# A two-layer scan, attention and experts kernel: last turns in two parts, two batches' experts packed, small sums in PSUM

## The chip, the cores and the metric

The kernel runs on one core of one Trainium2 chip. What is compared is the device time of one launch, in microseconds (us), as a median of several executions. A traced execution gives the profile: when each instruction of the five engines ran, what it waited for, and which transfers were under way. The engines are called PE (matrix multiply), DVE (vector), ACT (scalar functions), POOL (GpSimd) and SP, which here only issues transfers. Each engine works through its own list of instructions in order; semaphores tie the lists together. All data is float32.

## What is computed

x has the shape (4, 384, 32, 32): 4 batches, 384 channels, 1024 positions. Layer 0 is a selective scan in four directions, layer 1 a windowed attention and a mixture of four experts:

```python
x = x + _L0_conv_ref(_gn(x), ...)          # group norm, then the scan layer
t = _to_tokens(x)                          # (4, 1024, 384)
t = t + _L1_attn_ref(_ln_t(t), ...)
t = t + _L1_ffn_ref(_ln_t(t), ...)
x = _from_tokens(t, x)

# the scan layer: positions by rows, by columns, and both reversed
xs = _cross_scan(x)
...
def step(h, inp):
    dtt, ut, bt, ct = inp
    dA = jnp.exp(dtt[..., None] * A)
    h = h * dA + (dtt * ut)[..., None] * bt[:, :, None, :]
    y = jnp.einsum('bkdn,bkn->bkd', h, ct)
    return (h, y)
...
# the experts: two of four for each token
topk_vals, topk_idx = jax.lax.top_k(probs, TOP_K)
...
h = jax.nn.gelu(jnp.einsum('bsd,edh->ebsh', x, w1) + b1[:, None, None, :], approximate=False)
y = jnp.einsum('ebsh,ehd->ebsd', h, w2) + b2[:, None, None, :]
out = jnp.einsum('bse,ebsd->bsd', masked, y)
```

The state has 16 values for each channel and direction, so a batch has 4 x 384 x 16 recurrences of 1024 steps. Attention has 6 heads of 64 and looks back 64 tokens. An expert is 384 to 1536 to 384.

## The kernel before

**A scan slot.** The scan is cut into turns, one for each batch and direction: 16 turns, four a batch, the directions in the order of `ORDER` (columns, columns reversed, rows, rows reversed). A turn has 3 channel tiles (`t`) of 4 blocks (`j`) of 32 channels; a block has four groups (`g`) of 4 states, so that 32 channels x 4 states fill the 128 partitions. One block and one group is a slot: 48 slots a turn, 768 in all. A slot is five steps on 128x1024 elements:

- `spread` loads the steps dt and dt*u of 32 channels, each row four times, from DRAM into `dts` and `dtu` (512 KB each, once for four slots), through SP.
- `times_b`, on POOL: z = spread of dt*u times the row of B. At most three slots ahead of the scan, with 7 buffers z.
- `decay`, on ACT: dA = exp(a * dt), into one of two dA buffers in PSUM.
- `scan`, on DVE: one tensor_tensor_scan over 1024 positions. Its result h goes over z or over dA.
- `times_c`: h times the row of C, on POOL where h is in z, on DVE where it is in dA. `scan` chooses: POOL, if the planner's clock of POOL is not more than 0.6 ahead of DVE's (`on_pool`).

`fold_y` sums over states on PE, for two blocks at once: 16 matmuls with `fold` (128x32) into ps_y, added to a row in DRAM (`ydr`). It gives the z buffers back.

**What feeds and follows it.** `group_norm(b)` normalizes batch b and projects it to the rows of dt, B and C; `time_steps` and `half_step` make softplus(dt) and dt*u for one channel tile at a time, at most 40 slots ahead. When all folds of a batch are in DRAM (`have.add(("scan", b))`), `tokens(b)` takes its eight tiles of 128 tokens, three at a time: y0, layer norm, gelu (ps_g), layer norm, q, k, v (ps_qk, ps_v), scores (ps_s), softmax, transposes (ps_p), ps_o, projection (ps_pr), and the experts' logits. Four tiles are a part; `route` then finds the two experts of each of its tokens, counts how many went to each expert, gives each token a row in `xsdr` by indirect transfers from POOL, and lists blocks of 128 rows with the expert of each. `SIZES` says how many blocks a part may list: 5 for the first of a batch, 14 for the second, 19 in all, since 2048 pairs of a token and an expert fill at most 16 + 3 blocks. `loads`, `hidden` and `output` run the blocks: 8 weight tiles of 576 KB each, 36 matmuls 128x128x128 (ps_hid), gelu on ACT, 12 matmuls with 384 columns (y_ff). When the 19 blocks of a batch are done, `combine(b)` gathers each token's two results (`cb<-ysdr`), weighs and adds them (ps_c) and writes the output.

**What sets the order.** Everything is a Python generator that is run once while the program is built. `Machine` keeps a planner's clock for each engine and a price for each instruction (`Engine.ask`), and always emits the one that could start first by its clock, with a bias: scan feed and tokens early, experts late. The order of each engine's list is fixed by this; waits on the chip are by semaphores. Weight tiles (`wts`, 8) and row tiles (`rows`, 10) are shared by tokens, experts and combining; `tokens` holds four weight tiles as long as it runs.

**Small steps.** `group_norm` keeps the means and deviations of its 3 columns in an SBUF tile `g`; `route` works on some 16 columns, most of them in a PSUM bank `ps_r`, some in SBUF (`p`, `r`, `total`, `done`, `start`).

The lines that the profile names are L148 for a single instruction (`Engine.run`) and L159 for one of a list (`Engine.all`), so groups go by tile names. The two that hold the choice of POOL or DVE, and when a batch's tokens may begin:

```python
on_pool = count_of["times"] >= min(s + AHEAD, NSLOT) and m.clock["pool"] < m.clock["dve"] + LEAD
...
folded[b] = folded.get(b, 0) + 2
if folded[b] == KG * NB:
    have.add(("scan", b))
```

Of the kernel before, what the change touches and what calls it, by code (L numbers as in the profile page):

```python
# [11 lines left out]
F32 = mybir.dt.float32  # L12
# [29 lines left out]
FULL = 2 * PT - NE + 1  # L42
SIZES = (FULL, 2 * NT + NE - 1 - FULL)
MB = max(SIZES)
SEG, SPARE = NT, NE * NT
# [91 lines left out]
class Engine:  # L137
# [23 lines left out]
    def ask(self, op, a, k):  # L161
# [25 lines left out]
        elif self.name == "act":  # L187
            cost = 0.08 + 0.00085 * n + 0.1 * sum(hasattr(k.get(v), "tensor") for v in ("bias", "scale"))
            cost += 0.19 if "accum_out" in k else 0.0
            table = TABLES.get(a[2]) if op == "activation" else None  # L190
        elif self.name == "pool":
            cost = 0.1 + 0.0022 * n
        elif self.name == "sp":
            cost = 1.5
        else:
            cost = 0.17 + 0.00198 * n if "scan" in op else 0.14 + 0.00105 * n
            if n < 256 and not any(v.space == PSUM for v in outs + ins):
                cost += 0.5
# [14 lines left out]
DMA_RATE, DMA_TIME = 0.38e6, 2.2  # L213


class Machine:
# [51 lines left out]
    def account(self, op, start):  # L268
# [18 lines left out]
        if op.size:  # L287
            self.dma = max(self.dma, end) + op.size / DMA_RATE
            end = max(end + DMA_TIME, self.dma + 1.0)
# [101 lines left out]
def conv_attn_hybrid(  # L391
# [16 lines left out]
    al_sb = const_load(alog, [P, KG, T, NS], "al_sb")  # L408
# [23 lines left out]
    minus = const.tile([P, P], F32, name="minus")  # L432
    nc.gpsimd.tensor_scalar(minus, ident, -1.0, None, ALU.mult)
# [47 lines left out]
    base_e = const.tile([P, NE], F32, name="base_e")  # L481
    a4 = const.tile([P, KG, T, JB, NG], F32, name="a4")

# [34 lines left out]
    own = tables[:, JB * P : JB * P + SG]  # L518
    nc.gpsimd.memset(sel_j, 1.0)
# [13 lines left out]
    xsdr = [dram.tile([(SPARE + 1) * P, D], F32, name="xsdr", tag=f"xs{n}", bufs=1) for n in range(2)]  # L533
    ysdr = [dram.tile([(SPARE + 1) * P, D], F32, name="ysdr", tag=f"ys{n}", bufs=1) for n in range(2)]
# [4 lines left out]
    ORDER = (1, 3, 0, 2)  # L539
# [3 lines left out]
    NSLOT = len(blocks) * NG  # L543
    SP = 2 * NG
    TS, IS = JB * NG, NB * NG
    AHEAD = 3
# [6 lines left out]
    def place_of(s):  # L553

        return s // SP * 2 + s % 2, s % SP // 2

# [14 lines left out]
    def constants():  # L571
# [5 lines left out]
        for j in range(JB):  # L577
# [4 lines left out]
                pv, sel_j[:, j, :], al_sb.rearrange("p k t n -> p (k t n)"), start=True, stop=True  # L582
# [17 lines left out]
        yield from dve.tensor_scalar(base_e, count[:, :NE], float(SEG), None, ALU.mult)  # L600

    def prepare():
# [23 lines left out]
        for xs in xsdr + ysdr:  # L626
            for mb in range(0, SPARE + 1, SEG):
                yield scans(n)
                n += 4
                k = min(SEG, SPARE + 1 - mb)  # L630
# [22 lines left out]
    def group_norm(b):  # L653
# [21 lines left out]
        g = rp.tile([P, 5, T], F32, tag="g", name="g", bufs=1)  # L675
        mean, g_mean, dev, g_rstd, g_off = (g[:, n, :] for n in range(5))
        yield from dve.tensor_copy(mean, mv[:, :, 0])
        gs = rp.tile([GROUPS, 2], F32, tag="gs", name="gs")
        ps = yield from banks.take("ps_gm", 0)
        for n, src in enumerate((mean, dev)):  # L680
            for t in range(T):
                yield from pe.matmul(
                    ps[:GROUPS, T : T + 1], gm[:, t, :], src[:, t : t + 1],
                    start=t == 0, stop=t == T - 1,
                )
            yield from dve.tensor_copy(gs[:, n : n + 1], ps[:GROUPS, T : T + 1])
            for o in range(T):
                yield from pe.matmul(
                    ps[:, o : o + 1], gt_sb[:, ts(o, P)], gs[:, n : n + 1], start=True, stop=True
                )  # L690
            if src is mean:
                yield from dve.tensor_copy(g_mean, ps[:, :T])
                yield from dve.tensor_tensor(dev, mean, g_mean, ALU.subtract)
                yield from dve.tensor_tensor(dev, dev, dev, ALU.mult)
                yield from dve.tensor_tensor(dev, dev, mv[:, :, 1], ALU.add)
        yield from dve.tensor_scalar(g_rstd, ps[:, :T], EPS, None, ALU.add)
        banks.give(ps)
# [985 lines left out]
```

## Time and profile before

| | |
|---|---|
| median of 3 runs | 3823.28 us (3820.04 to 3826.16) |
| the profiled execution | 3807.62 us, span 3805.9 us |
| busy PE, DVE, POOL, ACT | 3060.2, 2906.1, 2795.4, 2217.3 us |
| first scan to last fold | 59 to 3088 us |
| last fold to the end | 3088 to 3806 us |
| transfers | 947 MB, 249 GB/s in the mean |

The span is what the engines took from the first to the last instruction; 1.7 us of the profiled execution lie outside it. Groups are listed as line, engine, operation, output and inputs, shape and count, then busy time, the mean of one in ns, and the idle time of the engine just before them. A PE matmul in float32 is two records in the trace. The trace was also read by stage: the scan of a batch (four turns) begins at 59, 719, 1529 and 2324 us, and the last fold ends at 3088 us.

### The profile page before, as it was taken

How to read it: one execution, taken by the hardware profiler on the slowest of the kernel's cores; microseconds unless marked ns; L12 is line 12 of the kernel's file. 1: busy time of each engine (PE TensorE's matmuls, PEld its weight loads, DVE VectorE, ACT ScalarE, POOL GpSimd, SP SyncE). 2: the span in 40 equal slices, each digit the busy share in tenths (PEclk: the TensorE clock that was granted, in tenths of full speed). 3: DMA queues.
4: the chain of work that ended last, by engine and by line, in shares of the span. 5: the costliest groups of instructions: out<-in, count | busy, mean ns of one | idle time of the engine just before them, and what ended most of it. 6: DMA issues, size and time to landing. Idle time of an engine off the chain costs nothing. (4 is left out here: it accounts for less than half of the span.)

```text
span 3805.9 us, 50657 instructions
## 1 busy us (share of the span) xinstructions
PE 3060.2 (80%) x16090; PEld 1880.4 (49%) x16090; DVE 2906.1 (76%) x3290; ACT 2217.3 (58%) x4020; POOL 2795.4 (73%) x1464
## 2 busy tenths in 40 slices
PE   5565565587888798877778888887988989999998
PEld 2111110155654455534444555555655568877886
DVE  5999999988799999898888999988898952421001
ACT  4455455476676677766566677877766645432221
POOL 4999989898789787999898799988999940101001
PEclk8666676688798899977788899988999999999997
DMA  6776684534488899754387889665789874479995
GB/s 212 278 276 233 247 309 145 195 117 156 167 299 333 299 370 332 287 171 141 122 283 257 299 310 361 218 235 179 239 286 365 312 232 142 142 243 345 313 318 188
DMA packets 392907, 947.32 MB, mean 249 GB/s; under 512 B 50848, under 2 KB 174616, under 8 KB 392640
## 3 DMA queue, kind: packets, MB, share of 16 engines
q1 hardware_dynamic: 381032, 918.51, 68.9%
q0 software_dynamic: 8192, 25.17, 1.9%
q8 instruction: 128, 2.10, 0.2%
q14 instruction: 139, 1.14, 0.1%
q10 hardware_dynamic: 3416, 0.41, 0.1%
HBM read 780.03 MB, written 182.78 MB: 253 GB/s over the span
## 5 line engine op out<-in xcount | busy, mean ns | idle before, releaser
L148 POOL TENSOR_TENSOR z<-dts,bc 128x1024 f32<-128x1024 f32 x768 | 1791.1, 2358 | 143.8 <-PE ps_y L159 90.8
L148 ACT ACTIVATE dA<-dts,a 128x1024 f32<-128x1024 f32 x768 | 854.9, 1118 | 536.5 <-DVE z L148 521.7
L148 DVE TENSOR_TENSOR_SCAN dA<-dA,z 128x1024 f32<-128x1024 f32 x421 | 963.0, 2287 | 77.3 <-ACT dA L148 55.1
L159 PE MATMUL ps_y<-z,fold 128*32 128x512 f32 x3072 | 658.3, 722 | 318.0 <-POOL z L148 184.3
L148 POOL TENSOR_TENSOR z<-z,bc 128x1024 f32<-128x1024 f32 x347 | 813.6, 2358 | 80.3 <-DVE z L148 72.3
L148 DVE TENSOR_TENSOR_SCAN z<-dA,z 128x1024 f32<-128x1024 f32 x347 | 779.6, 2276 | 33.2 <-ACT dA L148 31.4
L159 PEld LDWEIGHTS ps_hid<-xbt,w_sb 128*128 128x128 f32 x5472 | 668.4, 198 | 139.5 <-issue 46.5
L159 PE MATMUL y_ff<-w_sb,hs 128*128 128x384 f32 x1824 | 691.1, 521 | 49.3 <-ACT hs L159 40.3
L159 PE MATMUL ps_hid<-xbt,w_sb 128*128 128x128 f32 x5472 | 690.8, 283 | 38.2 <-issue 10.3
L148 DVE TENSOR_TENSOR z<-dA,bc 128x1024 f32<-128x1024 f32 x421 | 514.2, 1221 | 18.4
L148 ACT ACTIVATE hs<-ps_hid,bb 128x128 f32<-128x128 f32 x912 | 273.6, 364 | 419.7 <-PE ps_hid L159 361.6
L159 PEld LDWEIGHTS y_ff<-w_sb,hs 128*128 128x128 f32 x1824 | 346.2, 202 | 309.4 <-ACT hs L159 72.9
L159 PEld LDWEIGHTS ps_y<-z,fold 128*32 128x32 f32 x3072 | 91.4, 117 | 678.0 <-POOL z L148 310.5
L148 POOL DMA_INDIRECT cb<-ysdr,idx x64 | 62.1, 970 | 338.0 <-DMA ysdr<-yb 259.0
L148 DVE COPY yb<-y_ff 128x384 f32<-128x384 f32 x24 | 13.4, 558 | 307.1 <-PE y_ff L159 297.0
L159 POOL TENSOR_TENSOR rn<-rn,half 128x1 f32<-128x1 f32 x96 | 52.8, 550 | 242.6 <-DVE rn L159 234.5
L148 POOL DMA_INDIRECT xsdr<-tks,idx x64 | 65.0, 1016 | 160.2 <-DMA xsdr<-tks,idx 66.7
L148 ACT ACTIVATE ed<-ps_dt,dtb_sb 128x512 f32<-128x512 f32 x192 | 123.1, 680 | 22.9 <-PE ps_dt L148 15.1
L148 ACT COPY ed<-ps_dt 128x512 f32<-128x512 f32 x96 | 56.1, 584 | 110.6 <-DVE ed L148 110.5
L148 PE MATMUL ps_dt<-xd,dtw_sb 12*128 12x512 f32 x180 | 108.3, 774 | 10.6 <-ACT tt L148 2.9
L159 PEld LDWEIGHTS ps_o<-v,pt 128*128 128x128 f32 (+1 forms) x720 | 104.6, 226 | 12.1 <-issue 2.3
L159 PE MATMUL ps_o<-v,pt 128*128 128x64 f32 (+1 forms) x720 | 109.0, 313 | 0.8 <-ACT v L148 0.5
(219 smaller groups left out, 3555.4 us busy)
## 6 DMA issues: line engine op xcount, KB each, us to landing
w_sb<-wl SPq DMA_DIRECT2D x608, 576.0 KB
dts<-dtr SPq DMA_DIRECT2D x384, 512.0 KB
bc<-xdr SPq DMA_DIRECT2D x128, 512.0 KB
dtr<-ed SPq DMA_DIRECT2D x192, 256.0 KB
yp<-ydr SPq DMA_DIRECT2D x96, 256.0 KB
ydr<-yp SPq DMA_DIRECT2D x96, 256.0 KB
ub<-udr SPq DMA_DIRECT2D x45, 512.0 KB
wl<-in_w_dram SPq DMA_DIRECT2D x32, 576.0 KB
```

The source lines that it names most:

```text
L148: return getattr(self.real, op)(*a, **k)
L159: getattr(self.real, op)(*a, **k)
```

## The change

Four things are changed, each told here with its lines.

1. **Last turns in two parts.** `ORDER` becomes (1, 3, 2, 0), so that the last turn of a batch runs forward over rows, and turns 7, 11 and 15 (`halved`: the last of batches two to four) are taken as two halves of 512 positions: all channel tiles and blocks for the first half, then all for the second. A slot is then two blocks of 32 channels side by side, 512 positions each; it has two loads, two exponentials and two scans, and in the first half the last value of each scan is copied to a `carry` tile, from which the second half starts. `have` now tells of halves, and a token tile waits for its own half only.

2. **Experts' blocks packed.** `PACKS` puts batches two and three together: their tokens' rows fill one set of blocks, so that 5 + 8 + 8 + 14 = 35 blocks are listed for both, 5 + 14 for each of the others. Both are combined when the 35 are done. The row buffers of the pack are twice as long.

3. **Small sums in PSUM.** In `group_norm` and `route` steps with two inputs in SBUF get one of them in PSUM.

4. **The planner's prices.** ACT, scans, POOL's powers, indirect transfers and small DVE steps with two SBUF inputs cost more in `ask` and `account`.

Besides, the first batch's softplus takes its sum with a negated second term, so that a negated identity isn't needed, and the A logs are loaded into a weight tile that is free at the start.

```diff
+PACKS = ((0,), (1, 2), (3,))
+PACK = {b: g for g, bs in enumerate(PACKS) for b in bs}
+SIZES = []
+for bs in PACKS:
+    for at in range(2 * len(bs)):
+        full = 2 * PT * (at + 1) + (NE - 1 if at == 2 * len(bs) - 1 else 1 - NE)
+        SIZES.append(full - (2 * PT * at + 1 - NE if at else 0))
...
-            cost = 0.08 + 0.00085 * n + 0.1 * sum(hasattr(k.get(v), "tensor") for v in ("bias", "scale"))
+            cost = 0.14 + 0.00085 * n + 0.1 * sum(hasattr(k.get(v), "tensor") for v in ("bias", "scale"))
...
-            cost = 0.1 + 0.0022 * n
+            cost = 0.7 if ALU.pow in a or ALU.pow in k.values() else 0.1 + 0.0022 * n
...
-            cost = 0.17 + 0.00198 * n if "scan" in op else 0.14 + 0.00105 * n
-            if n < 256 and not any(v.space == PSUM for v in outs + ins):
-                cost += 0.5
+            cost = 0.26 + 0.00198 * n if "scan" in op else 0.14 + 0.00105 * n
+            if n < 512 and "scan" not in op and sum(v.space != PSUM for v in ins) > 1 and not any(v.space == PSUM for v in ins):
+                cost += 1.2
...
-            end = max(end + DMA_TIME, self.dma + 1.0)
+            late = DMA_TIME if e != "pool" else SCATTER if str(op.outs[0].space).endswith("DRAM") else GATHER
+            end = max(end + late, self.dma + 1.0)
...
-    ORDER = (1, 3, 0, 2)
+    ORDER = (1, 3, 2, 0)
...
+    halves = [(c, t, j) for c in range(NH) for t in range(T) for j in range(0, JB, 2)]
+    halved = (7,11,15)
...
-            yield from dve.tensor_copy(gs[:, n : n + 1], ps[:GROUPS, T : T + 1])
+            yield from dve.tensor_copy(gs[:, n : n + 1], ps[:GROUPS, 3 * T + n : 3 * T + n + 1])
...
-                yield from dve.tensor_tensor(dev, mean, g_mean, ALU.subtract)
-                yield from dve.tensor_tensor(dev, dev, dev, ALU.mult)
-                yield from dve.tensor_tensor(dev, dev, mv[:, :, 1], ALU.add)
+                mm.tensor_tensor(off, mv[:, :, 0], g_mean, ALU.subtract)
+                mm.tensor_tensor(dev, mv[:, :, 0], g_mean, ALU.subtract)
+                mm.tensor_tensor(off, off, dev, ALU.mult)
+                mm.tensor_tensor(dev, mv[:, :, 1], off, ALU.add)
...
+                for o in range(2):
+                    r = slice(32 * (j + o), 32 * (j + o) + 32)
+                    yield from sp.dma_start(
+                        dst[:, ts(o, HB)],
+                        dtrs[i, t][c, r, ts(hf, HB)].unsqueeze(1).to_broadcast([32, SG, HB]),
+                    )
...
-            yield from act.activation(
-                da, spreads[n, 0], AF.Exp, scale=a4[:, turns[i][1], t, j, g : g + 1]
-            )
+            for o in range(1 if hf is None else 2):
+                c = slice(0, L) if hf is None else ts(o, HB)
+                yield from act.activation(
+                    da[:, c], spreads[n, 0][:, c], AF.Exp,
+                    scale=a4[:, turns[i][1], t, j + o, g : g + 1],
+                )
...
+        if hf == 0:
+            yield from eng.tensor_copy(kept(n, g), pairs(h)[:, :, HB - 1 : HB])
+        yield from eng.tensor_tensor(view(zs[s], hf), view(h, hf), rows_of(i, g, 1, hf), ALU.mult)
...
+            if hf is not None:
+                for o in range(2):
+                    c = ts(o, HB)
+                    initial = kept(n, g)[:, o, :] if hf else 0.0
+                    yield from dve.tensor_tensor_scan(h[:, c], da[:, c], z[:, c], initial, ALU.mult, ALU.add)
...
+        for c in range(NH):
+            if folded[b, None] == whole and (whole == KG * NB // 2 or folded.get((b, c), 0) == NB // 4):
+                have.add(("scan", b, c))
...
         def tile(a):
+            yield lambda: ("scan", b, a // PT) in have
...
-        mm.tensor_reduce(r, p, AX.X, ALU.max)
-        mm.tensor_tensor(pp, p, bcast_last(r, NE), ALU.subtract)
+        mm.tensor_reduce(rr, p, AX.X, ALU.max)
+        mm.tensor_tensor(pp, p, bcast_last(rr, NE), ALU.subtract)
...
-        left[b] = left.get(b, 0) + 1
-        if left[b] == sum(SIZES):
-            have.add(("experts", b))
+        left[g] = left.get(g, 0) + 1
+        if left[g] == 2 * NT * len(PACKS[g]) + NE - 1:
+            for b in PACKS[g]:
+                have.add(("experts", b))
...
-            yield lambda: b < KEEP or ("out", b - KEEP) in have
+            yield lambda: PACK[b] < KEEP or all(("out", c) in have for c in PACKS[PACK[b] - KEEP])
```

## The prediction

> **What bounds the kernel now.** I read the page's slices first, then busy time by stage, then the groups by line, then who waits for whom.
>
> ```profile
> PE   5565565587888798877778888887988989999998
> DVE  5999999988799999898888999988898952421001
> ACT  4455455476676677766566677877766645432221
> POOL 4999989898789787999898799988999940101001
> PEclk8666676688798899977788899988999999999997
> ```
>
> The right third tells most: VectorE and GpSimd are nearly full for about 32 of the 40 slices and then empty, while TensorE stays at nine tenths to the end. So there are two stages one behind the other. I cut them at the end of the scan and at the two routing sums of the last batch. Columns: busy us and number of instructions of PE, PEld, DVE, ACT and POOL, then granted clock, DMA share, GB/s.
>
> ```profile
> 59.00:719.00 660.00, 396.94 (x1056) 85.50 (x1056) 632.33 (x402) 336.30 (x393) 609.53 (x266) 0.68 0.69 245
> 719.00:1529.00 810.00, 673.18 (x3607) 419.36 (x3604) 722.98 (x797) 558.02 (x999) 684.42 (x346) 0.85 0.71 256
> 1529.00:2324.00 795.00, 623.74 (x3298) 382.21 (x3296) 712.91 (x803) 532.07 (x938) 714.86 (x368) 0.84 0.68 241
> 2324.00:3088.00 764.00, 658.66 (x3843) 428.89 (x3835) 689.02 (x770) 546.42 (x1001) 708.65 (x365) 0.93 0.77 266
> 3088.00:3276.00 188.00, 178.51 (x1215) 148.42 (x1214) 56.04 (x221) 86.54 (x242) 11.76 (x32) 0.97 0.48 151
> 3276.00:3378.00 102.00, 94.84 (x619) 78.64 (x618) 35.91 (x156) 42.40 (x112) 14.02 (x24) 0.95 0.58 187
> 3378.00:3500.00 122.00, 111.85 (x699) 90.98 (x699) 16.70 (x61) 29.15 (x96) 19.81 (x21) 0.94 0.94 335
> 3500.00:3700.00 200.00, 200.00 (x1231) 160.48 (x1232) 10.90 (x20) 48.15 (x159) 3.11 (x4) 1.00 0.93 317
> ```
>
> The first four rows are the four batches' scans (four turns each, 192 slots), 3027 us together: DVE and POOL about 90% each, PE 78%. From 3088 on PE does what is left: it is busy 93 to 100%, for 718 us. So a microsecond of PE work taken out of the second stage is worth nearly a microsecond; in the first, PE work is worth something only where the folds of z come late. The groups (busy us, mean ns | idle us before them, who ended it), of GpSimd:
>
> ```profile
> L148 POOL TENSOR_TENSOR z<-dts,bc 128x1024 f32<-128x1024 f32 x768 | 1791.1, 2358 | 143.8 <-PE ps_y L159 90.8 <-DMA dts<-dtr 34.5 <-issue 5.7
> ```
>
> and of VectorE, shape by shape:
>
> ```profile
> L148 DVE TENSOR_TENSOR_SCAN dA<-dA,z 128x1024 f32<-128x1024 f32 x421 | 963.0, 2287 | 77.3 <-ACT dA L148 55.1 <-POOL z L148 20.8 <-issue 1.1
> ...
> L148 DVE TENSOR_TENSOR z<-dA,bc 128x1024 f32<-128x1024 f32 x421 | 514.2, 1221 | 18.4
> L148 DVE TENSOR_TENSOR ps_dt<-ps_dt,ed 128x512 f32<-128x512 f32 x144 | 99.4, 691 | 10.3 <-ACT ps_dt L148 8.4
> ...
> L159 DVE TENSOR_TENSOR ps_r<-p,r 128x16 f32<-128x16 f32 x8 | 9.5, 1183 | 0.6
> ...
> L159 DVE TENSOR_TENSOR ps_r<-ps_r,r 128x16 f32<-128x16 f32 x8 | 1.5, 182 | 0.3
> ```
>
> These are the prices of a slot, and a comparison: the same 16 elements take 1183 ns when both inputs lie in SBUF and 182 ns when one is in PSUM. The waits of the scan stage:
>
> ```profile
> POOL z L148 <- PE ps_y L159: 92.0, 41, 8.6
> ...
> DVE dA L148 <- ACT dA L148: 55.1, 44, 4.3
> ...
> DVE z L148 <- ACT dA L148: 31.4, 30, 3.5
> ```
>
> **What the Trainium skill says.** "SBUF — State Buffer", section "Who interferes with whom": a VectorE instruction with two SBUF inputs contends with a GpSimd instruction that reads SBUF, and the later one waits. The trace agrees: ps_r<-p,r took 424 to 2316 ns in its six runs beside the scan and 183 ns in its two after it. "VectorE: DVE Perf Modes", section "The TRN2 errata — SBUF-src ops pay a fixed extra latency per instruction": the cost is per instruction, so halves cost more than a whole. The trace has no 512-element scan, but its multiplies agree: 2 x 691 - 1221 = 161 ns. "TensorE: Matmul & The Clock Gate", section "What's actually happening": a PE kept busy gets its full clock; here 0.68 in the first row and 1.00 in 3500:3700.
>
> **The change, part by part.** The counts come from setting the two programs' instruction orders side by side, engine by engine.
>
> *Tail, packed experts.* The diff's SIZES give 19 + 35 + 19 = 73 blocks of experts for 76: each batch alone rounds up with three spare blocks, the pair needs them once. The blocks of batches two and three are also nearer done when the scan ends: after the last fold the old order has 30 blocks' output sums (y_ff), the new one 23. A block is 36 ps_hid and 12 y_ff matmuls; after 3088 the trace has 254.3 us for 1044 and 256.9 us for 360 of these, so 0.244 and 0.714 us each. Gone: 252 x 0.244 + 84 x 0.714 = 121 us. Given back: both packed batches are combined there, 24 tiles for 16, so 48 more ps_c matmuls at 40.5/96 us: +20 us, and 8 transposes, +2.
>
> *Tail, last turn in two parts.* The first four token tiles of a batch may start when the first half of its last turn is folded. Of the last batch, three tiles stand ahead of the last fold up to their scores' inputs: 9 each of ps_y, ps_g, ps_x, ps_t, 27 each of both ps_qk, 6 ps_v, some ps_s, ps_p and ps_o go from the tail. Summing all 1864 matmuls that are left (2288 before) at the tail's own prices I get 604 us, against 741 us for the old list. The old list took 717.7 us (3088.2 to 3805.9; groups overlap at their seams), so 0.969 of its sum: 604 x 0.969 = 585 us. The tail loses 133 us. Against that stands filler: up to the last routing sum the old order has 8 blocks between the token tiles, the new 6, and the tiles' chains (norms over DVE, POOL, ACT) then show more. Unknown from the trace: at least 0; at most 50, if a fifth of the 249 us up to there goes idle, three times today's share. I take 15. Tail: -118 us.
>
> *Scan, VectorE.* 144 of 768 scans are now two of 512: nothing if all cost is per element, at most 46 us if the fixed part is twice the multiplies' 0.161, which is the nearest row and which I take: 144 x 0.161 = +23. The second halves read their start from a one-column SBUF operand: the row cb<-cb,gate,ps_c, which has such an operand too, takes 603 ns beside POOL and 614 after it, so no port wait; nothing. 41 copies of the end values on DVE at 154 ns (total<-ps_r): +6. 18 multiplies by C fewer at 1.221: -22. Small sums in PSUM: the 24 two-SBUF steps of group norm and routing in the scan stage took 43.8 us one by one; at 0.17 each they are 4: -40. Eight combine tiles fewer (605 + 551 ns): -9. Three tiles' fronts more: +12. Sum -30.
>
> *Scan, GpSimd.* 19 multiplies more at 2.358: +45; 31 end copies at 0.19 (as rn<-rn): +6; 16 gathers fewer at 0.97: -16; norms of three tiles: +4. Sum +39. C multiplies are handed to whichever of the two engines is behind, so the mean counts: (+39 - 30)/2 = +5, at 90% busy +6.
>
> *Scan, other queues.* ACT: 144 x (2 x 0.632 - 1.118) = +21, 51 more gelu inputs at 0.364 = +19, ten table loads at 1.283 = +13; it is 65 to 72% busy in turns 4 to 15, and hidden. SP: spreads become 144 loads of half the size for 72; no wait of SP for itself shows in POOL's z row beyond the start. PE: 6664 matmuls up to the last fold for 6405; turns 8 to 11 go from 1790 to 2027, where turns 12 to 15, with 2066, were the fastest of the three loaded stages (764 us). So PE work is hidden there, unless folds come late. The time steps' feed: all three row blocks of a halved turn are wanted in its first half; they are prepared 40 slots ahead, so nothing. For the finer pieces' hops I add 4. What truer durations in the ordering bring cannot be priced: at best the scan runs at 92.5% for 90% busy, 60 us of the 2369 in rows two to four (row one runs at 96%); at worst it costs what C or D below cost. I take nothing. Scan: +10.
>
> *Start and end.* The A logs' load moves behind the other constants on ACT, the first slot waits for the spread at 59 us; 0 to +5, taken 0. The last eight tiles' combine is as before.
>
> Sum: span 3805.9 - 118 + 10 = 3698. The profiled execution took 3807.6, the median of the runs is 15.7 above it. So 3698 + 1.7 + 15.7 = **3715 us**.
>
> **The rivals.** A (the forecast): the tail gives 118, the scan holds. For it: PE was full in the tail and its list is 19% shorter, whatever the clock does. Against: the scan is four fifths of the time and every order in it is new.
> B: the scan gains too, since small steps no longer wait for the port and the order fits the durations; 60 us, so 3655. For: DVE and POOL idle 10% though neither lacks work. Against: the POOL multiplies rise.
> C: folds come late where PE is denser. 259 more matmuls in the scan at 0.348 us (623.74/1790) are 90 us; if two thirds of that reach POOL through full z buffers (92.0 us of such waits today), 60 us: 3775.
> D, slower: the halved turns starve the scan. In turns 7, 11 and 15 each slot needs two exponentials from ACT, and now token fronts with their gelu table loads stand in ACT's queue in the same turns; behind a scan that waits are its multiply by C, the release of one of only two dA buffers, and PE's fold. A wait for dA lasts 86.5/74 = 1.17 us today. It decides from 0.75 us on each of the 144 slots, 108 us, or 92 slots that wait as long as today's mean; with all of them waiting it is 168 us, so 3715 + 168 = 3883, with three quarters 3841. For: such waits exist. Against: turn 5, with a full load of tokens, shows no such loss.
> That the change does nothing is excluded by the order: three tiles stand ahead of the last fold.
>
> **How the numbers follow.** A 0.57, B 0.22, C 0.13, D 0.08. A measurement tells about 0.2% (8 us) from no change; a sliver of C and D falls within it, 0.02. Faster 0.90, same 0.02, slower 0.08. A's own bounds are -15 and +35 in the tail, -20 and +30 in the scan; the range takes in B and C but for their outer ends: 3640 to 3795.
>
> **What would show it.** Last scan near 3095 and 600 us behind it; 73 blocks, 23 of them after; ps_r<-p in PSUM under 0.2 us; 512-element scans of 1.2 to 1.3 us; POOL z near 366 second multiplies. Wrong if the last scan ends after 3200, if turns 7, 11 and 15 grow by more than 20 us each beyond their token work, or if PE idles over 50 us between the last fold and the last routing sum.

## The result, and the profile after

The changed kernel takes 3758.7 us (median of 4 runs, 3749.3 to 3764.8) against 3821.7 us (4 runs, 3808.4 to 3826.2): 0.984 of the time, 95% interval 0.981 to 0.987. It is faster by 63 us; the forecast was 107. Between the two traced executions the difference is only 45 us (spans of 3805.9 and 3761.2 us): the one before lay 15.7 us under the median that the forecast used, the one after 4 us above its own. What follows is read from the traces. The slices after, to set beside those of before:

```profile
PE   5655565578788887998886887878888879998997
DVE  5999999999889877979898977898789976422001
ACT  4445454477677767776775666766678666432221
POOL 4999979998899878987998878888799995022001
PEclk8666676578799998988886888888999989999997
```

Look at DVE and POOL: their full stretches end about one slice later than before, and DVE's has more sevens in it (seven among slices 9 to 33, where before had one). The second stage is shorter. The same cuts as for the kernel before, at the first scan of each batch and at the last fold (from and to, length; then busy us and instructions of PE, PEld, DVE, ACT and POOL; clock, DMA share, GB/s):

```profile
59.00:717.00 658.00, 381.86 (x1050) 81.94 (x1048) 617.26 (x394) 336.79 (x391) 619.66 (x271) 0.67 0.76 263
717.00:1535.00 818.00, 672.92 (x3681) 422.23 (x3682) 709.03 (x885) 584.96 (x1083) 717.87 (x381) 0.87 0.72 254
1535.00:2371.00 836.00, 690.32 (x3715) 426.75 (x3713) 715.63 (x877) 581.95 (x1072) 714.00 (x376) 0.86 0.75 256
2371.00:3169.00 798.00, 674.72 (x3823) 434.02 (x3823) 683.28 (x817) 554.93 (x1046) 703.18 (x363) 0.88 0.71 247
3169.00:3761.00 592.00, 547.27 (x3424) 445.19 (x3420) 126.96 (x452) 180.71 (x523) 75.08 (x100) 0.94 0.72 240
```

The tail fell from 718 to 592 us. The scan stage grew from 3029 to 3110 us, in the three loaded batches from 810, 795 and 764 to 818, 836 and 798. Adding up DVE's busy time over the four scan rows gives 2725 us for 2757: DVE works 32 us less and the stage is 81 us longer, so it idles 113 us more. By turns, cut at DVE's scans (turn 15 ends with its last scan, some 5 us ahead of the last fold; the tail is the last fold to the end):

| us | before | after |
|---|---|---|
| turns 0-3 | 660 | 659 |
| turns 4-6 | 629 | 593 |
| turn 7 (halved) | 181 | 225 |
| turns 8-10 | 608 | 608 |
| turn 11 (halved) | 187 | 227 |
| turns 12-14 | 604 | 601 |
| turn 15 (halved) | 158 | 192 |
| tail | 718 | 592 |

The halved turns lost 44, 40 and 34 us, 118 together, and turns 4 to 6 gained 36. The prices of single instructions came as expected; the groups of VectorE, shape by shape:

```profile
L155 DVE TENSOR_TENSOR_SCAN dA<-dA,z 128x1024 f32<-128x1024 f32 x332 | 759.3, 2287 | 78.4 <-ACT dA L155 57.0 <-POOL z L155 15.5 <-issue 5.6
...
L155 DVE TENSOR_TENSOR z<-dA,bc 128x1024 f32<-128x1024 f32 x402 | 490.7, 1221 | 17.0 <-DVE dA L155 0.5
L155 DVE TENSOR_TENSOR_SCAN z<-dA,carry,z 128x512 f32<-128x512 f32 x86 | 105.3, 1267 | 11.4 <-ACT dA L155 11.4
L155 DVE TENSOR_TENSOR_SCAN dA<-dA,z 128x512 f32<-128x512 f32 x82 | 100.4, 1225 | 18.9 <-ACT dA L155 12.8 <-issue 4.8
...
L155 DVE TENSOR_TENSOR_SCAN dA<-dA,carry,z 128x512 f32<-128x512 f32 x58 | 74.6, 1286 | 27.6 <-ACT dA L155 21.1 <-issue 5.7
L155 DVE TENSOR_TENSOR_SCAN z<-dA,z 128x512 f32<-128x512 f32 x62 | 71.3, 1203 | 13.6 <-ACT dA L155 10.1 <-POOL z L155 3.5
...
L166 DVE TENSOR_TENSOR ps_r<-ps_r,p 128x16 f32<-128x16 f32 x16 | 2.9, 182 | 0.6
```

A half scan takes 1203 to 1286 ns where a whole one takes 2275 to 2287, and a 16-element step with one input in PSUM 182 ns, where ps_r<-p,r took 1183. The waits moved (waited for: us in total, times, longest):

```profile
POOL z L155 <- PE ps_y L166: 96.7, 44, 7.0
DVE dA L155 <- ACT dA L155: 90.8, 50, 8.8
DVE ed L155 <- ACT ps_dt L155: 67.1, 34, 8.7
DVE z L155 <- ACT dA L155: 43.0, 34, 6.3
```

POOL waits for folds about as long as before (96.7 us for 92.0), so folds did not come late. DVE waits for ACT's dA 134 us for 86, and for its softplus steps 67 for 27. That points to ACT; e12 below puts it to the test.

### The profile page after: what moved, and what is told of

It reads as the page before. It is cut to its first block, busy times and chain, and to the rows that moved or that the text cites. A ratio compares the mean times of both kernels' runs of the same rounds, so it can differ in the third digit from the quotient of the medians.

```text
span 3761.2 us, 50316 instructions
## 1 busy us (share of the span) xinstructions
PE 3002.3 (80%) x15769; PEld 1826.0 (49%) x15769; DVE 2870.2 (76%) x3467; ACT 2259.9 (60%) x4144; POOL 2843.6 (76%) x1513
## 5 line engine op out<-in xcount | busy, mean ns | idle before, releaser
L155 ACT ACTIVATE dA<-dts,a 128x1024 f32<-128x1024 f32 (+1 forms) x912 | 892.9, 983 | 478.5 <-DVE z L155 452.7
L155 DVE TENSOR_TENSOR_SCAN dA<-dA,z 128x1024 f32<-128x1024 f32 (+1 forms) x414 | 859.7, 2077 | 97.3 <-ACT dA L155 69.7
L155 POOL TENSOR_TENSOR z<-z,bc 128x1024 f32<-128x1024 f32 x366 | 858.4, 2357 | 96.3 <-DVE z L155 78.7
L155 DVE TENSOR_TENSOR_SCAN z<-dA,z 128x1024 f32<-128x1024 f32 (+1 forms) x354 | 727.8, 2087 | 37.4 <-ACT dA L155 31.5
L166 PEld LDWEIGHTS ps_hid<-xbt,w_sb 128*128 128x128 f32 x5256 | 646.6, 200 | 136.4 <-issue 50.1
L166 PE MATMUL y_ff<-w_sb,hs 128*128 128x384 f32 x1752 | 675.5, 527 | 44.6 <-ACT hs L166 35.0
L166 PE MATMUL ps_hid<-xbt,w_sb 128*128 128x128 f32 x5256 | 667.4, 285 | 41.1 <-DMA w_sb<-wl 9.7
L155 DVE TENSOR_TENSOR z<-dA,bc 128x1024 f32<-128x1024 f32 x402 | 490.7, 1221 | 17.0 <-DVE dA L155 0.5
L155 DVE SCALAR_TENSOR_TENSOR ed<-ps_dt,ed 128x512 f32<-128x512 f32 x96 | 65.3, 681 | 67.4 <-ACT ps_dt L155 67.1
L155 DVE TENSOR_TENSOR_SCAN z<-dA,carry,z 128x512 f32<-128x512 f32 x86 | 105.3, 1267 | 11.4 <-ACT dA L155 11.4
```

What stands on the lines that cost most here:

```text
L155: return getattr(self.real, op)(*a, **k)
L166: getattr(self.real, op)(*a, **k)
```

## The experiments

Twelve kernels ran. Time is the median of the timed runs, and the ratio to the kernel before is given as its 95% interval. When the last fold comes and how long the tail and the turns (4 to 6, 7 and so on) last is read from one traced execution each:

| | time, us | ratio | last fold | tail | 4-6 | 7 | 8-10 | 11 | 12-14 | 15 |
|---|---|---|---|---|---|---|---|---|---|---|
| e1 no halves | 3730.5 | 0.974-0.979 | 3039 | 698 | 589 | 181 | 597 | 190 | 608 | 152 |
| e2 whole tokens | 3780.1 | 0.988-0.993 | 3080 | 691 | 590 | 215 | 595 | 210 | 588 | 161 |
| e3 last only | 3750.7 | 0.981-0.986 | 3080 | 660 | 584 | 180 | 598 | 188 | 612 | 194 |
| e4 no packs | 3771.4 | 0.986-0.990 | 3172 | 599 | 592 | 230 | 602 | 229 | 610 | 189 |
| e5 no halves, old prices | 3752.8 | 0.980-0.985 | 3056 | 690 | 591 | 180 | 612 | 184 | 608 | 155 |
| e6 before, new prices | 3834.0 | 1.003-1.006 | 3101 | 716 | 617 | 178 | 612 | 200 | 605 | 162 |
| e7 before, sums in PSUM | 3746.7 | 0.978-0.984 | 3052 | 692 | 602 | 170 | 614 | 181 | 602 | 162 |
| e8 split spreads | 3718.5 | 0.970-0.977 | 3031 | 686 | 583 | 171 | 614 | 172 | 610 | 159 |
| e9 split engines | 3766.6 | 0.984-0.989 | 3072 | 700 | 588 | 194 | 607 | 203 | 595 | 163 |
| e10 LEAD 0.61 | 3758.6 | 0.983-0.987 | 3032 | 721 | 610 | 175 | 595 | 191 | 590 | 158 |
| e11 one pack of three | 3740.1 | 0.978-0.982 | 3029 | 709 | 599 | 173 | 595 | 187 | 602 | 153 |
| e12 whole exponentials | 3739.8 | 0.977-0.980 | 3156 | 587 | 588 | 224 | 606 | 225 | 604 | 188 |

The control first, because it says what the others are worth.

**e10: another order alone.** e1 with `-LEAD = 0.6` / `+LEAD = 0.61`.

> A control: the change without its halved turns, where only the margin by which GpSimd takes a multiply is 0.61 us instead of 0.60. No instruction's work changes, only the order that the planner finds. It says how far a last fold and a tail move by another order alone, and so which of the differences of the other runs carry a reading. The order's list for the tail says 714 us against 692. If orders matter little: tail 715 to 722, last fold 3030 to 3050, time 3745 to 3765. If they matter: single turns move by 10 to 20 us against the same version at 0.60 and the last fold by up to 20.

Against e1 the last fold moved by 7 us, single halved turns by up to 6, a group of three turns by up to 21, the tail by 23, the time by 28. (PE's list for the tail, the matmuls that the order leaves behind the last fold at the prediction's prices, had said 22 for the tail.) So a difference of some 20 to 30 us in the time of two versions shows nothing by itself here; this is one control, and another order may move more. Below I rest on the last fold, on all three halved turns going one way, or on larger differences.

**e1, e2, e3: what the halves do.** e1 is the changed kernel with no halved turn:

```diff
-    halved = (7,11,15)
+    halved = ()
```

> No turn is halved; packing, PSUM sums and new prices stay. In the changed kernel's trace the last fold is at 3168 us (3088 before), turns 7, 11 and 15 took 225, 227 and 192 us (181, 187 and 158 before), turns 4 to 6 593 (630 before). The order has 2215 matmuls behind the last fold, 692 us at the tail's prices. Theory 1 (half turns cost about 40 us each in the scan, whatever the reason, and prices and PSUM sums give about 35 in turns 4 to 6 and as much later): last fold near 3050, time 3740 to 3755, below the changed kernel or level with it. Rival (the scan stage is longer because PE holds more experts' work or because of the new prices, not because of the halves): last fold stays above 3120, time 3810 or more.

e2 halves the turns but lets a batch's tokens begin only when both parts are folded:

```diff
-            yield lambda: ("scan", b, 0) in have
+            yield lambda: ("scan", b, 0) in have and ("scan", b, 1) in have
```

> The three turns are halved, but a batch's tokens wait for both halves, so that no token front stands in a halved turn. Order: 692 us behind the last fold. Theory 1a (the halved turns are slow because tokens start in their middle: four weight tiles and the tiles' rows are loaded among the spreads, the experts' rows land late, PE waits in order and ACT and DVE behind it): turns 7, 11, 15 fall to 190, 195 and 165 us, last fold near 3060 to 3080, time 3755 to 3775. Theory 1b (halving itself is slow: two exponentials, two scans, copies and hops for each slot): the turns stay at 215 or more, last fold above 3120, time 3815 or more.

e3 halves only the last turn (`halved = (15,)`).

> Only turn 15 is halved. Order: 672 us behind the last fold, turns 8 to 11 hold 1720 matmuls as without halves (1981 in the changed kernel), two tiles' fronts ahead of the last fold. Theory 1: turns 7 and 11 back near 185 us, turn 15 near 190; last fold near 3085, time 3750 to 3765. If the gain of the tail came from the last batch's own early tiles, as the prediction had it, the tail would be near 600 us; the order says 672, so that most of it comes from turns 7 and 11.

Halves gain nothing. e1, without them, takes 3730.5 us, with an interval below that of the changed kernel; e10, also without them, takes 3758.6, as the changed kernel does. So whether they lose on the time is within the reach of an order. On the last fold they do lose: 3039 us in e1 and 3032 in e10 for 3169. Halving alone (e2 over e1) costs 34, 20 and 9 us in the three turns, of which turns 12 to 14 give 20 back, and leaves the tail about as it was: 41 us on the last fold, 50 on the time (33 between the two traces). Theory 1 of e1 came true on the last fold (3039 us, near 3050). Neither theory of e2 holds as it was put: both the halves and the fronts cost. Letting token fronts into the halved turns (changed kernel over e2) takes 99 us out of the tail and puts 89 in front of it, in turns 7 to 15. e3 shows the same exchange in one turn: 42 us more in turn 15, 38 less in the tail. So of the 106 us between the tails of e1 and the changed kernel some 38 come with turn 15, and the rest with turns 7 and 11. What busy time says of the exchange: e1 in its three last turns, and below it the changed kernel in its own.

```profile
1305.00:1486.00 181.00, 167.47 (x885) 99.10 (x883) 163.86 (x110) 132.61 (x222) 150.81 (x65) 0.94 0.93 348
2083.00:2273.00 190.00, 148.63 (x796) 87.06 (x796) 176.94 (x190) 119.30 (x198) 173.56 (x84) 0.86 0.80 291
2881.00:3033.00 152.00, 135.22 (x777) 83.36 (x775) 144.22 (x84) 98.77 (x160) 151.47 (x67) 0.94 0.81 293
```

```profile
1311.00:1535.00 224.00, 184.05 (x995) 113.47 (x994) 173.50 (x205) 158.92 (x307) 180.40 (x99) 0.92 0.86 289
2144.00:2371.00 227.00, 181.79 (x939) 110.68 (x935) 176.82 (x209) 157.32 (x302) 172.37 (x94) 0.89 0.79 264
2971.00:3163.00 192.00, 156.70 (x901) 100.82 (x901) 156.03 (x181) 126.45 (x253) 166.64 (x93) 0.89 0.72 234
```

Before halving, DVE is busy 91 to 95% of these turns, PE 78 to 93% and POOL 83 to nearly 100%. There is little room for more work. After it no engine reaches 88%: in the three turns ACT has 92 us more to do, PE 71, POOL 44 and DVE 21, and they last 120 us longer. The rest is waiting.

**e4: packs.** `PACKS = ((0,), (1,), (2,), (3,))` in the changed kernel.

> Each batch lists its own blocks again (76), the rest as changed. Order: 599 us behind the last fold (585 with packs), 2098 matmuls in turns 12 to 15 for 2024. Theory: packing is worth about 14 us of the tail and the scan hardly changes: last fold 3160 to 3185, time 3765 to 3790. Rival (packing is worth its three blocks of 17 us): 3800 or more. Second rival (packing worth nothing, since 16 combines are put into the tail): 3750 to 3762.

The tail is 599 us for 592, the last fold 3172 for 3169, the time 3771.4 for 3758.7. The pack is worth some 13 us, less than an order moves; the 126 us of the tail do not come from it.

**e5, e6, e7: what made turns 4 to 6 shorter.** e5 is e1 with the old prices and DMA times in the planner, e6 the kernel before with the new ones. The lines of e6 for DVE; those for ACT, POOL's powers and the transfers are the change's own:

```diff
-            cost = 0.17 + 0.00198 * n if "scan" in op else 0.14 + 0.00105 * n
-            if n < 256 and not any(v.space == PSUM for v in outs + ins):
-                cost += 0.5
+            cost = 0.26 + 0.00198 * n if "scan" in op else 0.14 + 0.00105 * n
+            if n < 512 and "scan" not in op and sum(v.space != PSUM for v in ins) > 1 and not any(v.space == PSUM for v in ins):
+                cost += 1.2
```

e7 is the kernel before with nothing but the small sums of `group_norm` and `route` in PSUM, of which the first lines are

```diff
-        g = rp.tile([P, 5, T], F32, tag="g", name="g", bufs=1)
-        mean, g_mean, dev, g_rstd, g_off = (g[:, n, :] for n in range(5))
+        g = rp.tile([P, 3, T], F32, tag="g", name="g", bufs=1)
+        dev, g_rstd, g_off = (g[:, n, :] for n in range(3))
```

> The change without its halved turns, with the prices of small steps and DMA waits that the kernel before had. Question: turns 4 to 6, which hold no halved work, took 629 us before, 593 after and 589 in the version without halves. What took the 36 to 40 us out: the prices (another order of the same work), or the small sums left in PSUM? Theory P (prices, which my prediction set at nothing): turns 4 to 6 go back to 620 to 635 and turns 8 to 10 with them; last fold 3070 to 3090 against 3039, tail 690 (the order's own list says 684, against 692 with the new prices), time 3765 to 3785. Theory S (sums in PSUM): turns 4 to 6 stay at 585 to 598, last fold 3035 to 3050, time 3725 to 3745.

> The kernel before with nothing but the new prices in the ordering. The complement of the run without them. Theory P (the prices made turns 4 to 6 shorter): turns 4 to 6 near 590 to 600, last fold 3040 to 3060, tail 718 as before or a little less (the order's list 714 against 718), time 3755 to 3785. Theory S (the sums): turns 4 to 6 stay at 620 to 635, last fold 3080 to 3100, time 3800 to 3830, no change.

> The kernel before with nothing but the small sums of the norm and of the routing left in PSUM. Theory S: turns 4 to 6 near 590 to 600, as in the changed kernel, last fold 3040 to 3055; the order's list for the tail says 681 against 718, so time 3730 to 3765. Theory P: turns 4 to 6 stay at 620 to 635, last fold 3075 to 3095, and only the tail's list (681) pays: 3775 to 3800.

The sums did it: e7 alone takes 36 us off the last fold and 71 off the time. DVE's busy time ahead of the last fold falls from 2758 to 2707 us, POOL's rises from 2718 to 2731. The gain does not hang on one order: the six versions with these sums and whole scans (e1, e5, e7, e8, e10, e11) have their last folds at 3029 to 3056 us and take 3719 to 3759 us; the two without the sums, the kernel before and e6, have 3088 and 3101 and take 3822 and 3834. Turns 4 to 6 alone (27 us in e7, where the control moved such a group by 21) and the tail (26 us, control 23) would not show it. With the old prices turns 4 to 6 stay at 591. The prices alone make the kernel before no faster (0.4% slower), their 12 us in turns 4 to 6 come back as 13 in turn 11; e5 and e1 differ by less than an order moves.

At 3746.7 us e7, one part of the change, is as fast as the whole (3758.7), within what an order moves.

**e8: are the halved loads slow?** e1, with the spreads of turns 7, 11 and 15 loaded in two column halves. The expectation speaks of dt's spreads alone; the edit has no such condition and halves those of dt*u too, so that the trace has 144 loads of 256 KB, as many as the changed kernel:

```diff
+                for h in range(2 if i in (7, 11, 15) else 1):
+                    cc = ts(h, HB) if i in (7, 11, 15) else slice(0, L)
+                    n_c = HB if i in (7, 11, 15) else L
+                    yield from sp.dma_start(
+                        dst[:, cc],
+                        dtrs[i, t][c, 32 * j : 32 * j + 32, cc].unsqueeze(1).to_broadcast([32, SG, n_c]),
+                    )
```

> The change without its halved turns, where only the spreads of the first multiplier (dt) in turns 7, 11 and 15 are loaded by two DMAs of 512 columns instead of one of 1024: 48 issues and 48 halves more, the same bytes, no scan halved. Question: turns 7, 11 and 15 lost 34, 20 and 9 us by halving alone. Theory D (the transfers: pieces of 2 KB instead of 4, twice the issues in SP's queue): this version loses 15 to 30 us in turn 7 and 8 to 18 in turn 11 against 181 and 190, time 3750 to 3775. Theory E (the engines' own halves: ACT's two exponentials, DVE's two scans, the carry, and POOL's added multiplies): turns 7, 11 and 15 within 8 us of 181, 190 and 152, time 3722 to 3745.

Turns 7 and 11 came out shorter, not longer (171 and 172 for 181 and 190), turn 15 by 7 longer, turns 8 to 10 by 17. The theory of slow small loads fell. At 3718.5 us this is the fastest version that ran, but its interval overlaps that of e1, and by the control the difference can be the order's.

**e9: are the halved instructions slow?** e1, with scans and exponentials of these turns in two halves each, and nothing else halved. The lines of the scan; the exponentials are divided in the same way:

```diff
-                yield from dve.tensor_tensor_scan(h, da, z, 0.0, ALU.mult, ALU.add)
+                for o in range(parts):
+                    c = ts(o, L // parts)
+                    initial = h[:, HB - 1 : HB] if o else 0.0
+                    yield from dve.tensor_tensor_scan(h[:, c], da[:, c], z[:, c], initial, ALU.mult, ALU.add)
```

> The change without its halved turns, where each exponential of ACT and each scan of DVE in turns 7, 11 and 15 is made in two instructions of 512 columns (the second scan starts from the first one's last column): the same blocks in the same order, no carry, loads of 1024 columns, and every result as before. Added from the durations of the trace: 48 x (2 x 0.70 - 1.12) = 13 us for ACT and 48 x (2 x 1.27 - 2.28) = 12 us for DVE in each of the three turns. Theory E (the halves on the engines cost what halving cost, 34, 20 and 9 us in turns 7, 11, 15): these turns grow by 12 to 30 us each over 181, 190 and 152, last fold 3065 to 3100, time 3740 to 3775 (the order's list for the tail is 681 against 692). Theory O (what costs is the other order of a halved turn: two columns' halves, rows for two blocks at once, fronts and waits that come another way): at most 8 us each, last fold 3030 to 3060, time 3715 to 3745.

Turns 7, 11 and 15 grew by 13, 13 and 11 us, the last fold by 33. The half scans of e9:

```profile
L155 DVE TENSOR_TENSOR_SCAN dA<-dA,z 128x512 f32<-128x512 f32 x158 | 198.7, 1258 | 26.3 <-ACT dA L155 21.4 <-POOL z L155 2.4
L155 DVE TENSOR_TENSOR_SCAN z<-dA,z 128x512 f32<-128x512 f32 x130 | 160.3, 1246 | 5.1 <-ACT dA L155 3.0
```

288 of them take 359 us, and 144 whole ones at 2.28 would take 328: 31 us of DVE time, nearly all of the 33. Theory E holds at its lower end, and of the 41 us that halving puts on the last fold this is most. The run halves the exponentials too, and ACT has 41 us more to do ahead of the last fold than in e1, so it does not part DVE's share from ACT's. That DVE's counts is argued from e1, where DVE was busy 91 to 95% of these turns and ACT 63 to 73%.

**e12: is ACT the pace of the halved turns?** The changed kernel with each engine's order kept, where ACT makes a halved slot's decay in one exponential:

```diff
-                yield from act.activation(
-                    da[:, c], spreads[n, 0][:, c], AF.Exp,
-                    scale=a4[:, turns[i][1], t, j + o, g : g + 1],
-                )
+                call = (da[:, c], spreads[n, 0][:, c], AF.Exp), dict(scale=a4[:, turns[i][1], t, j + o, g : g + 1])
+                yield act.ask("activation", *call)
...
+                elif o:
+                    act.real.activation(da, spreads[n, 0], AF.Exp, **call[1])
```

> The changed kernel with its halved turns, token fronts and packs, and each engine's order of work kept instruction for instruction, except that ACT makes the decay of a halved slot in one exponential of 1024 columns instead of two of 512 (with the first block's scale for both, so the second block's decays are left out). It takes 48 x (2 x 0.70 - 1.12) = 13 us from ACT in each of turns 7, 11 and 15 and touches nothing else. Question: which engine's queue sets the pace of the halved turns, where DVE waited for ACT's dA and dt 29, 33 and 20 us. Theory ACT (ACT's one queue, which holds exponentials, dt steps and the token fronts' steps with two buffers for dA, is what the scan waits for): each halved turn gives back 9 to 15 us of 225, 227 and 192, last fold 3125 to 3145 against 3169, time 3715 to 3735. Theory PE/DVE (the halved scans on DVE, or PE's queue with its waits for loads, set the pace; ACT's lateness is only what came last): at most 5 us each, last fold 3155 to 3170, time 3745 to 3765.

(The A of this input is the same for all channels, so both blocks have the same scale and, unlike what the expectation says, nothing is left out.) The three turns:

```profile
1305.00:1529.00 224.00, 187.74 (x1012) 116.67 (x1010) 174.08 (x206) 148.61 (x261) 183.14 (x100) 0.91 0.85 289
2134.50:2359.00 224.50, 180.99 (x941) 110.07 (x939) 177.30 (x209) 146.18 (x254) 172.58 (x93) 0.90 0.79 268
2963.00:3151.00 188.00, 155.68 (x902) 100.87 (x903) 155.91 (x181) 115.47 (x207) 165.73 (x93) 0.90 0.73 240
```

ACT is relieved of 10 to 11 us in each and the turns last 224, 225 and 188 us for 225, 227 and 192. Theory ACT fell as far as the second exponentials go; ACT's other steps in these turns, those of the token fronts, no run took out. The time itself is 19 us lower than the changed kernel's, more than the other theory allowed; the traces place 7 of it in these turns, and the other differences (5 in turns 4 to 6, 5 in the tail, where the two kernels do the same) are not explained.

The waits, added up over the three turns, say where the relief went:

| us | e1 | e2 | after | e12 |
|---|---|---|---|---|
| DVE waits for ACT | 23 | 65 | 92 | 91 |
| ACT waits for PE | 32 | 70 | 111 | 138 |
| PE waits for transfers | 10 | 22 | 57 | 54 |

With less to do, ACT waited longer for PE, and DVE as long for ACT as before. ACT was the last to arrive; the waits fit that it stood behind PE, but no run shows it.

PE's own waits by what was waited for, in turn 15 of the changed kernel, and then of e2:

```profile
PE ps_xb L166 <- DMA xb<-xsdr: 14.5, 3, 8.2
PE ps_y L166 <- POOL z L155: 6.8, 4, 3.0
PE ps_y L166 <- DMA tt<-in_x_dram: 6.7, 1, 6.7
```

```profile
PE ps_y L166 <- POOL z L155: 14.3, 9, 3.1
PE y_ff L166 <- ACT hs L166: 3.9, 3, 1.4
PE ps_xb L166 <- DMA xb<-xsdr: 3.1, 1, 3.1
```

With token fronts in the turn PE stands 21 us for two loads, 3 without. The one of xb is issued among those of wq, wk and wv, 576 KB each. That fits the 31 us that fronts add to turn 15, but no run took these loads away, and turn 11 shows no such growth (4.9 us for xb, as in e2). What holds up the fronts there stays open.

**e11: a better pack?** e8 (its halved loads are again those of both spreads) with `PACKS = ((0,), (1, 2, 3))`.

> A version that may beat both kernels: no halved turns, dt's spreads of turns 7, 11 and 15 loaded in two halves (as in the run that had 3718 us), and the experts' blocks of batches one, two and three in one pack instead of two. Two blocks' worth of padding less after the last fold: the order's list for the tail says 627 us against 681. If the pack works as the other packs did (12 us for the change's pack by the run without packs, 54 here by the list): tail 630 to 640, last fold 3020 to 3050, time 3655 to 3690. Rival: the pack holds batch two's blocks back until batch three's routing, they pile up behind the last fold in spite of the list, or a larger segment makes the gathers wait: tail above 665, time above 3700.

The rival came true: the tail is 709 us for 627 by its list, though only 70 blocks are listed for 73. The first 300 us of the tail of e11 and of e8:

```profile
3029.00:3130.00 101.00, 89.20 (x542) 72.06 (x543) 31.96 (x122) 37.47 (x106) 8.88 (x24) 0.87 0.29 89
3130.00:3230.00 100.00, 81.31 (x501) 70.20 (x501) 44.79 (x201) 40.19 (x114) 15.57 (x28) 0.79 0.21 70
3230.00:3330.00 100.00, 82.76 (x542) 68.94 (x541) 21.52 (x100) 28.43 (x83) 9.25 (x12) 0.90 0.60 216
```

```profile
3031.00:3130.00 99.00, 90.72 (x600) 74.63 (x600) 24.35 (x95) 37.56 (x110) 5.19 (x14) 0.97 0.56 177
3130.00:3230.00 100.00, 96.06 (x691) 81.36 (x690) 44.86 (x193) 53.84 (x139) 10.21 (x24) 1.00 0.52 164
3230.00:3330.00 100.00, 90.49 (x600) 77.03 (x598) 33.15 (x145) 37.67 (x102) 15.41 (x24) 0.93 0.61 195
```

In the first 200 us of e11's tail far less is loaded than in e8's (89 and 70 GB/s for 177 and 164), and PE does fewer matmuls. It idles 48 us in the 300, for 22 in e8, at a granted clock of 0.79 to 0.90. Experts' work between the token steps, the filler, is missing, and the token steps' matmuls are slower as well (ps_t 332 ns for 277 in e8, ps_pr 309 for 276), those of the experts not (ps_hid 282 for 288).

## Why the prediction was half right

*The total.* 3758.7 us lies in the range, with some luck. By spans the forecast missed by 63 us (3761 for 3698), by medians by 44, because the traced executions lay on different sides of their medians. The tail came as forecast, the scan stage 71 us worse.

*Tail, -118 us: right in size.* Measured -126. PE's list for the tail and its length agree within 19 us in eleven versions out of twelve:

| us | before | after | e1 | e2 | e3 | e4 | e5 | e6 | e7 | e8 | e9 | e10 | e11 |
|---|---|---|---|---|---|---|---|---|---|---|---|---|---|
| by the list | (fitted) | 585 | 692 | 692 | 672 | 599 | 684 | 714 | 681 | 681 | 681 | 714 | 627 |
| measured | 718 | 592 | 698 | 691 | 660 | 599 | 690 | 716 | 692 | 686 | 700 | 721 | 709 |

The 15 us for thinner filler did not come. From the last fold to the last routing sum PE idles 15 us (3169 to 3414 us), and idled 17 in that stretch of the kernel before (3088 to 3379), far from the 50 that would have spoken against the forecast:

```profile
3088.00:3379.00 291.00, 274.35 (x1840) 228.06 (x1839) 92.46 (x380) 128.94 (x353) 25.78 (x56) 0.96 0.52 164
3169.00:3414.00 245.00, 230.27 (x1551) 189.92 (x1547) 92.42 (x362) 106.08 (x283) 46.29 (x70) 0.97 0.59 186
```

The cause was named wrong. The text gave most of the gain to the packed experts and the rest to three fronts of the last batch. e4 shows the packs nearly without part in it: what did it is the token fronts in the halved turns. They stand ahead of the last fold themselves and start the experts earlier (23 blocks are left for e2's 27.7; with packs and no halves, in e1, it is also 27.7, and without packs, in e7, 28.0), and that is the 99 us between e2 and the changed kernel. Another 26 lie between the kernel before and e7, which an order alone could move.

*Busy time in the scan stage: right, but for ACT.* DVE -32 us for -30, POOL 2755 - 2718 = +37 for +39, the second multiplies 366 as said, half scans 1.20 to 1.29 us for 1.2 to 1.3. PE's work before the last fold grew by 67 us for the 90 of rival C, ACT's by 86 for 53; half exponentials cost more than was taken. Small slips of the working change nothing: its first four rows add up to 3029 us, not 3027, and DVE lost 19 multiplies by C, not 18.

*From busy time to length: the step that failed.* "The mean counts ... at 90% busy, +6", with ACT, PE and SP "hidden", gave +10. The stage grew by 81, with DVE's work down. The mean of DVE and POOL hid two things of opposite sign. What the sums take off DVE paid nearly in full: 36 us off the last fold (e7) for a sum of 40. And what halves add in turns 7, 11 and 15, where DVE is 91 to 95% busy, counts in full (e9: 31 us of DVE work, 33 of length, with ACT's share not parted), where the mean left half of it. The large term is the token fronts, priced at +12 on DVE and at nothing on PE: 89 us. From e2 to the changed kernel PE's busy time ahead of the last fold grows by 77 us, ACT's by 56, DVE's by 19. "PE work is hidden there" was read from the batches' means (PE 78 to 86% busy), but the fronts come in the batches' last turns, where 58 of the 89 us fell (10, 17 and 31); 26 fell in the turns between. The other terms from version to version: prices, packs and the rest without halves -13 (e1 over e7), the order of a halved turn beyond its instructions +8 (e2 over e9). Together -36 - 13 + 33 + 8 + 89 = 81. As steps from one version to the next they must add up; the two small ones are about what an order moves by itself. Why the fronts cost nearly all that they save, the runs do not settle; they show that it is so, and that PE, ACT and DVE wait behind each other there.

*The rivals.* C, late folds, did not come: POOL waits for them 97 us for 92. Of B, the small steps gave 36 us, more than the mean had left of them, and the prices nothing (e6). D had the right place and, on the turns alone, the right size: 118 us on 144 slots is 0.82 us on each, above its threshold of 0.75. It gave the loss to late dA, by second exponentials and token fronts in ACT's queue. e12 takes the second exponentials out and gains 7 us in these turns; that the token fronts cost is shown, that they do so in ACT's queue is not, and the waits speak for PE's. The total is faster nevertheless since turns 4 to 6 and the tail gave more. The text held against D that turn 5, full of tokens, shows no loss. The trace shows that turn with 230 us, the longest of the 16, and with DVE busy 85%: a turn with room is no witness for one that has none.

*The sign shown beforehand* for being wrong, turns 7, 11 and 15 each more than 20 us longer beyond their token work, came true for two of them: with the fronts they are 44, 40 and 34 us longer than before, and without (e2) 34, 23 and 3. The last scan ended at 3163 us, not near 3095, and not after the 3200 of the other sign.

## What to carry to other kernels

Work taken forward out of a full tail is a gain only where it lands in room; read the room from the very stretch it lands in, not from a stage's mean, and ask for a version without the move: here the other parts of the change alone gave 3730.5 us and, in another order, 3758.6, the whole 3758.7, and the small sums by themselves 3746.7. A list of one engine's work predicts a stage's length only as long as filler keeps that engine full. Where a planner rewrites the order, run a control that changes only the order before reading anything from 20 us.

## What was not expected of the hardware

Two half scans cost 0.17 us more than a whole one in the changed kernel (2 x 1.221 - 2.269, busy time over number, all forms), where 0.161 was taken from the multiplies, and 0.21 in e9. A half that starts from the carry column took 1267 and 1286 ns, one that starts from 0.0 took 1203 and 1225: some 60 ns that the prediction put at nothing. Half exponentials cost 0.27 more (2 x 0.692 - 1.118), where another ACT operation of 512 columns (632 ns) had suggested 0.15. Over 100 us in which PE was busy 81% the mean granted clock was 0.79 (e11), and over 100 us at 96% it was 1.00 (e8).
